# Two adjacency products of a graph layer as Strassen's seven half-size products, with features on partitions

## The chip, the cores and the metric

One core of a Trainium2 chip. The metric is device time of one execution in microseconds (us). "The profile" is a page that sums up one profiled execution. "The trace" is the record behind it, asked by views: groups of instructions, timeline, busy time by windows, waits. Times such as 1536.40 are us from the start of the profiled span.

## The reference

Two pre-norm residual layers over the rows of `x` [3327, 512] with an adjacency `adj` [3327, 3327], all in float32. Layer 0 is attention with `adj` added to the scores. The change is in layer 1:

```python
h = relu(layernorm(x1))
A2 = adj + eye(N)
s = diag(A2) ** -0.5
temp = A2 @ h @ W.T                       # first adjacency product, then the weights
out = x1 + relu((s[:, None] * A2 * s[None, :]) @ temp)    # second adjacency product
```

Each adjacency product is 3327 x 3327 by 3327 x 512. I call them convolution 1 and convolution 2.

## The kernel before

Layer 1 reads 128 x 512 tiles of the transposed adjacency from DRAM and never holds more than twelve of them. Its right sides, `h1` and `ts`, stay on chip. Convolution 1 leaves features on partitions; convolution 2 leaves rows on partitions, so its result goes straight to the output.

```python
def chunk(j, b, diagonal):                # A2^T[row tile j, column block b]
    a = conv.tile([P, BW], F32, name="a", bufs=12)
    load(a[:m, :wd], adjT[j * P : j * P + m, b * BW : b * BW + wd], m)
    ...                                   # + identity on the diagonal blocks
# (A2 h1)^T
for b in range(NB):
    acc = [psum.tile([P, BW], F32, name="mm", bufs=4) for _ in range(DC)]
    for j in range(NT):
        a = chunk(j, b, True)
        for d in range(DC):
            nc.tensor.matmul(acc[d][:, :wd], h1(j)[:, d, :], a[:m, :wd],       # L300
                             start=j == 0, stop=j == NT - 1)
        if j == 1 and waiting:
            temp(*waiting)                # ts of the block before, hidden in this one
    ...
# S A2 ts, and the residual
for b in range(NB):
    ...
    for j in range(NT):
        a = chunk(j, b, False)
        for t, i in enumerate(its):
            nc.tensor.matmul(acc[t][:n], a[:m, t * P : t * P + n], ts[j][:m],  # L324
                             start=j == 0, stop=j == NT - 1)
    ...
    for t, i in enumerate(its):           # scale and relu, residual, store
        ...
        store(out[i * P : i * P + n], r[:n], n)
```

Everything the second stage needs is on chip when the first ends, and the weights product `temp` of each block hides among the matmuls of the next. That is why TensorE hardly ever stops.

Of the kernel before, what the change touches and what calls it, by code (L numbers as in the profile page):

```python
# [9 lines left out]
F32 = mybir.dt.float32  # L10
# [5 lines left out]
BW = 512  # columns of a block: four row tiles, one PSUM bank of float32  # L16
# [4 lines left out]
def graph_layers_kernel(  # L21
# [4 lines left out]
    adjT: bass.AP,  # L26
# [6 lines left out]
    w1T: bass.AP,  # L33
    out: bass.AP,
):
    """Two pre-norm residual layers over the rows of x [N, D].

    Layer 0: x1 = x + softmax(q k^T / sqrt(D) + adj + adj) v, with h = relu(layernorm(x)).
    Layer 1: out = x1 + relu(S A2 S (A2 h1 W^T)), with A2 = adj + I, S = diag(A2)^-1/2.

    adjT and w*T are the transposes of adj and the weights; bq and bk come as [128, D / 128].
    All matrix products are in float32.
    """
# [3 lines left out]
    NT = (N + P - 1) // P  # row tiles  # L47
    NB = (N + BW - 1) // BW  # blocks of four row tiles
    TB = BW // P
    scale = 1.0 / math.sqrt(D)  # L50
# [10 lines left out]
    def pieces(n):  # L61
        # a DMA spreads over 16 engines only if 16 divides its partitions
        m = n - n % 16
        return [(0, m), (m, n)] if m and m < n else [(0, n)]
# [10 lines left out]
    held = ctx.enter_context(tc.tile_pool(name="held", bufs=1))  # L75
    work = ctx.enter_context(tc.tile_pool(name="work", bufs=2))
# [12 lines left out]
    # Per block, in turn: h^T of layer 0, q^T (scaled), h of layer 1. All three take  # L89
    # [128, 4, 128] for each row tile, and a row tile's earlier content is dead when the  # L90
    # next one is written.
# [3 lines left out]
    def h1(i):  # L95
        b, t = divmod(i, TB)
        return qh[b][: rows(i), :, t * P : (t + 1) * P]

    x1d = [dram.tile([rows(i), D], F32, name=f"x1d{i}") for i in range(NT)]

    def layernorm(dst, src, n):
        """dst = (src - mean) / sqrt(var + eps) along the row"""
# [10 lines left out]
    with tc.tile_pool(name="kv", bufs=1) as kv:  # L113
# [65 lines left out]
        S = {}  # L179

        def scores(i):
            """exp(a - max a) for the rows of tile i, in chunks of BW keys, and their negated max and sums"""
# [48 lines left out]
        def attend(i):  # L231
# [13 lines left out]
            y = work.tile([P, D], F32, name="y", bufs=1)  # L245
            layernorm(y[:n], xt[:n], n)
            nc.scalar.activation(h1(i), y[:n].rearrange("p (c e) -> p c e", c=DC), AF.Relu)
# [7 lines left out]
        att.close()  # L255

# [1 line left out]
    with tc.tile_pool(name="conv", bufs=1) as conv:  # L258
        w1 = conv.tile([P, DC, D], F32, name="w1")
        nc.sync.dma_start(w1, w1T.rearrange("(c p) o -> p c o", p=P))  # L260
        ts = [conv.tile([P, D], F32, name=f"ts{i}") for i in range(NT)]
        dg = [conv.tile([P, 1], F32, name=f"dg{i}") for i in range(NT)]
        sd = [conv.tile([P, 1], F32, name=f"sd{i}") for i in range(NT)]

        def chunk(j, b, diagonal):
            """A2^T[j-th row tile, b-th column block]"""
            m, wd = rows(j), width(b)
            a = conv.tile([P, BW], F32, name="a", bufs=12)
            load(a[:m, :wd], adjT[j * P : j * P + m, b * BW : b * BW + wd], m)
            if j // TB == b:  # L270
                t = j % TB
                blk = a[:m, t * P : t * P + m]
                nc.vector.tensor_add(blk, blk, ident[:m, :m])  # L273
                if diagonal:
                    junk = conv.tile([P, P], F32, name="junk", bufs=2)
# [3 lines left out]
            return a  # L279

        def temp(b, axt):
            """ts = S (A2 h1) W^T for the row tiles of block b"""
            for i in tiles_of(b):
                n, t = rows(i), i % TB
                ps = psum.tile([P, D], F32, name="av")
# [87 lines left out]
```

## Time and profile before

| | kernel before |
|---|---|
| time, median (lowest to highest, 4 runs) | 2798.26 us (2797.49 to 2799.17) |
| span of the profiled run | 2796.5 us |
| TensorE busy | 99% |
| convolution 1 starts / last matmul ends | 1536.4 / 2788.4 us |

The page, the seam between the layers and the end are shown in the prediction below. Windows over most of each convolution, kernel before; the columns are the stretch, its length, busy us (and count of instructions) of PE, PEld, DVE, ACT and POOL, then TensorE's clock, the DMA share and GB/s:

```profile
1600.00:2150.00 550.00, 550.00 (x1291) 245.35 (x1290) 35.40 (x93) 7.02 (x12) 10.96 (x20) 1.00 0.25 64
2210.00:2750.00 540.00, 540.00 (x1259) 239.33 (x1258) 23.85 (x46) 16.49 (x24) 13.03 (x24) 1.00 0.33 93
```

TensorE is busy in every microsecond at full clock. VectorE does 35 us of work in 550, and DMA is three quarters idle. The change wants to spend those idle resources to take work off TensorE.

### The profile page before, as it was taken

To read this page: it belongs to the slowest core of one execution; us is meant where nothing else is said; L and a number is where in the kernel's file an instruction comes from. 1 tells how busy PE (TensorE), PEld (TensorE's weight loads), DVE (VectorE), ACT (ScalarE), POOL (GpSimd) and SP (SyncE) were. 2 spreads that over 40 slices of the span, in tenths; PEclk is the share of its full clock that TensorE was granted. 3 is DMA by queue.
4 is the path that set the end of the run, shared out by engine and by line. 5 is a ranking of instruction groups with operands and counts; after the bars stand their busy time and mean duration, and the time that the engine had idled before them with its cause. 6 is when DMAs were issued, how large, how long until landed. Compare 5 with 4: busy or idle time off the path is not lost.

```text
span 2796.5 us, 18243 instructions
## 1 busy us (share of the span) xinstructions
PE 2770.7 (99%) x7260; PEld 1311.6 (47%) x7260; DVE 500.5 (18%) x979; ACT 255.7 (9%) x615; POOL 74.5 (3%) x138
## 2 busy tenths in 40 slices
PE   8999999999999999999998999999999999999998
PEld 4444544444444444454444444444445644444443
DVE  4121323232323232323222000000000000000000
ACT  1110111111111112121211000000000000000000
POOL 1000000000000000000000000000000000000000
PEclk9999999999999999999999999999999999999999
DMA  3000211111111211111111422222221332333322
GB/s 117 15 23 0 65 49 43 53 40 53 43 49 40 57 40 55 42 52 45 51 45 42 127 64 68 68 64 64 72 63 40 90 108 75 108 106 105 85 81 60
DMA packets 97045, 172.56 MB, mean 62 GB/s; under 512 B 11578, under 2 KB 21559, under 8 KB 96960
## 3 DMA queue, kind: packets, MB, share of 16 engines
q1 hardware_dynamic: 92736, 157.77, 20.5%
q0 software_dynamic: 4224, 13.63, 1.3%
q8 instruction: 57, 0.93, 0.1%
q14 instruction: 28, 0.23, 0.0%
HBM read 157.73 MB, written 13.63 MB: 61 GB/s over the span
## 4 chain that ended last, share of the span: by engine, by line
PE 99%; DMA 1%; DVE 0%; SPq 0%; ACT 0%; POOL 0%; issue 0%; POOLq 0%; ACTq 0%
PE mm L300 21%; PE av L242 21%; PE mm L198 21%; PE mm L324 21%; PE mm L158 6%; PE av L287 3%; PE av L151 3%; PE tp L223 3%; DMA xt<-in_x_dram 0%; PE tp L142 0%; DMA a<-in_adjT_dram 0%; DVE st L104 0%; DVE xt L111 0%; SPq L68 0%; ACT pT L225 0%
## 5 line engine op out<-in xcount | busy, mean ns | idle before, releaser
L242 PE MATMUL av<-v,pT 128*128 128x512 f32 (+2 forms) x1352 | 606.3, 593 | 0.6 <-ACT pT L225 0.6
L300 PE MATMUL mm<-a,qh 128*128 128x512 f32 (+3 forms) x1456 | 583.4, 563 | 7.6 <-DVE a L273 7.6
L198 PE MATMUL mm<-kT,qh 128*128 128x512 f32 (+3 forms) x1456 | 588.5, 562 | 0.0
L324 PE MATMUL mm<-ts,a 128*128 128x512 f32 (+2 forms) x1352 | 580.6, 592 | 0.0
L300 PEld LDWEIGHTS mm<-a,qh 128*128 128x128 f32 (+1 forms) x1456 | 277.7, 191 | 313.1 <-issue 307.6
L198 PEld LDWEIGHTS mm<-kT,qh 128*128 128x128 f32 (+1 forms) x1456 | 274.8, 190 | 302.6 <-issue 298.4
L324 PEld LDWEIGHTS mm<-ts,a 128*128 128x128 f32 (+2 forms) x1352 | 257.2, 190 | 322.7 <-issue 322.6
L242 PEld LDWEIGHTS av<-v,pT 128*128 128x128 f32 (+2 forms) x1352 | 246.8, 190 | 261.1 <-issue 253.8
L200 DVE SCALAR_TENSOR_TENSOR s<-s,mm 128x512 f32<-128x512 f32 (+2 forms) x182 | 118.2, 649 | 262.3 <-PE mm L198 262.3
L225 ACT COPY pT<-tp 128x512 f32<-128x512 f32 (+1 forms) x104 | 51.9, 499 | 819.2 <-PE tp L223 819.2
L208 ACT ACTIVATE s<-s,nmx 128x512 f32<-128x512 f32 (+2 forms) x182 | 123.2, 678 | 30.9 <-DVE nmx L204 30.2
L202 DVE TENSOR_REDUCE mx<-s 128x1 f32<-128x512 f32 (+2 forms) x182 | 117.9, 648 | 6.2
L223 PEld LDWEIGHTS tp<-ident,s 128*128 128x128 f32 (+2 forms) x676 | 84.8, 142 | 71.6 <-issue 68.8
L273 DVE TENSOR_TENSOR a<-a,ident 128x128 f32<-128x128 f32 (+1 forms) x52 | 15.2, 292 | 524.1 <-DMA a<-in_adjT_dram 432.9
L225 DVE COPY pT<-tp 128x512 f32<-128x512 f32 (+1 forms) x78 | 53.7, 688 | 269.6 <-PE tp L223 269.6
L223 PE MATMUL tp<-ident,s 128*128 128x128 f32 (+2 forms) x676 | 99.3, 273 | 0.0
L151 PE MATMUL av<-wv,qh 128*128 128x512 f32 (+1 forms) x208 | 93.1, 598 | 0.0
L158 PE MATMUL mm<-qh,wk 128*128 128x512 f32 (+1 forms) x224 | 90.4, 562 | 0.0
L158 PE MATMUL mm<-qh,wq 128*128 128x512 f32 (+1 forms) x224 | 90.4, 562 | 0.0
L287 PE MATMUL av<-w,axt 128*128 128x512 f32 (+1 forms) x208 | 90.4, 592 | 0.0
L332 ACT ACTIVATE r<-mm,sd 128x512 f32<-128x512 f32 (+1 forms) x26 | 17.9, 687 | 570.1 <-PE mm L324 570.1
L333 DVE TENSOR_TENSOR r<-r,x 128x512 f32<-128x512 f32 (+1 forms) x26 | 18.0, 693 | 283.8 <-ACT r L332 283.8
(40 smaller groups left out, 555.8 us busy)
## 6 DMA issues: line engine op xcount, KB each, us to landing
a<-in_adjT_dram SPq DMA_DIRECT2D x300, 256.0 KB, 2.7
s<-in_adj_dram SPq DMA_DIRECT2D x150, 256.0 KB, 2.7
xt<-in_x_dram SPq DMA_DIRECT2D x25, 256.0 KB, 3.3
xr<-in_x_dram SPq DMA_DIRECT2D x25, 256.0 KB, 2.7
x1d<-xr POOLq DMA_DIRECT2D x25, 256.0 KB, 2.3
x<-x1d SPq DMA_DIRECT2D x25, 256.0 KB, 4.1
out_dram<-r POOLq DMA_DIRECT2D x25, 256.0 KB, 5.1
a<-in_adjT_dram SPq DMA_DIRECT2D x50, 127.5 KB, 2.0
```

Source lines behind the costliest of these rows:

```text
L151: nc.tensor.matmul(ps[:n], qh[b][:, c, t * P : t * P + n], w["v"][:, c, :], start=c == 0, stop=c == DC - 1)
L158: nc.tensor.matmul(ps[:, :wd], w[nm][:, c, o * P : (o + 1) * P], qh[b][:, c, :wd], start=c == 0, stop=c == DC - 1)
L198: nc.tensor.matmul(ps[:n, :wd], qh[qb][:, d, t * P : t * P + n], kT[c][:, d, :], start=d == 0, stop=d == DC - 1)
L200: nc.vector.scalar_tensor_tensor(ch[c][:n, :wd], ch[c][:n, :wd], 2.0, ps[:n, :wd], op0=ALU.mult, op1=ALU.add)
L202: nc.vector.reduce_max(mx[:n, c : c + 1], ch[c][:n, :wd], axis=AX.X)
L208: nc.scalar.activation(ch[c][:n, :wd], ch[c][:n, :wd], AF.Exp, bias=nmx[:n], accum_out=sums[:n, c : c + 1])
L223: nc.tensor.transpose(pt[:m, k, :n], S[i][0][c][:n, k * P : k * P + m], ident[:n, :n])
L225: cp(sb[:, :full, :n], pt[:, :full, :n])
L242: nc.tensor.matmul(ps[:n], now[:m, k, :n], v[j][:m], start=j == 0, stop=j == NT - 1)
L287: nc.tensor.matmul(ps[:n], axt[:, d, t * P : t * P + n], w1[:, d, :], start=d == 0, stop=d == DC - 1)
L300: nc.tensor.matmul(acc[d][:, :wd], h1(j)[:, d, :], a[:m, :wd], start=j == 0, stop=j == NT - 1)
L324: nc.tensor.matmul(acc[t][:n], a[:m, t * P : t * P + n], ts[j][:m], start=j == 0, stop=j == NT - 1)
```

## The change

Pad N to 3328 and cut the matrices into quarters. Strassen's scheme then needs seven products of half size for eight, at the price of sums of the operands. VectorE makes those sums. The rows of the result are done in four strips of 416 columns per half. `adjq` is the padded transpose, cut on the host so that a strip of a quarter is contiguous. The diagonal, too, now comes cut from the host (`dg`); the kernel before took it from its tiles with VectorE. The time of the host is not measured. Features are on partitions in both convolutions, so convolution 2's result must be turned back. A right side is now needed as whole quarters before the first product can start, so `h1`, `ts` and both results go through DRAM.

```diff
-        def chunk(j, b, diagonal): ...
+        Y = {r: conv.tile([P, HT, HD], F32, name=f"y{r}") for r in range(1, 8)}
+        def right_sides(src):
+            for r, J, d in ((5, 1, 1), (2, 0, 0), (6, 0, 1), (3, 0, 1), (7, 1, 0), (4, 1, 0)):
+                nc.sync.dma_start(Y[r], quarter(src, J, d))
+            nc.vector.tensor_add(Y[6], Y[6], Y[2])
+            nc.vector.tensor_add(Y[1], Y[2], Y[5])
+            nc.vector.tensor_sub(Y[3], Y[3], Y[5])
+            nc.vector.tensor_add(Y[7], Y[7], Y[5])
+            nc.vector.tensor_sub(Y[4], Y[4], Y[2])
+        def strip(I, J, ch):          # 416 columns of a quarter, in four groups of row tiles
+            ... a = conv.tile([P, GMAX, CW], F32, name="a", bufs=10) ...
+        def combine(op, to, by):      # VectorE, group by group
+            ...
+        def product(xs, r):           # 2 x 13 matmuls, 416 wide
+            ... nc.tensor.matmul(acc[:, :CW], Y[r][:, g, d * P : (d + 1) * P], a[:, g - g0, :], ...)
+        def convolve(outT, after_first):
+            for ch in range(CH):
+                a11 = strip(0, 0, ch)
+                x = strip(0, 1, ch); combine(ALU.add, x, a11);      m = product(x, 5) ...
+                if ch > 0: after_first(ch)
+                x = strip(1, 0, ch); combine(ALU.subtract, x, a11); m = product(x, 6) ...
+                x = strip(1, 1, ch); combine(ALU.add, x, a11);      m = product(x, 1) ...
+                m = product(a11, 3) ...
+                ...                    # 7, 2 and 4 likewise, around a22
+        right_sides(h1d)
+        convolve(y1T, lambda ch: None)
+        for i in [*range(HT, NT), *range(HT)]:      # temp: now a stage of its own
+            o = columns_of(y1T, i) ...               # load, 4 matmuls with w1, scale
+            nc.gpsimd.dma_start(tsd[i * P : (i + 1) * P], t)
+        right_sides(tsd)
+        def finish(ch):                              # turn back the row tiles of a strip
+            ... o = columns_of(y2T, i)               # 3 buffers "ot"; "x1" and "r" have 2
+            ... nc.tensor.transpose(pt[:, d, :], o[:, d, :], ident) ...
+        convolve(y2T, lambda ch: finish(ch - 1))
+        finish(CH - 1)
```

(Joined and cut. `h1` of layer 0 now goes to `h1d`, a store from the GpSimd queue.)

More of the change, by code (lines that the diff above doesn't have):

```diff
@@ L25, in graph_layers_kernel @@
     adj: bass.AP,
-    adjT: bass.AP,
+    adjq: bass.AP,
     wqT: bass.AP,
@@ L33, in graph_layers_kernel @@
     w1T: bass.AP,
+    dg: bass.AP,
     out: bass.AP,
@@ L49, in graph_layers_kernel @@
     TB = BW // P
+    NP = NT * P
+    HT = NT // 2
+    HN = HT * P
+    HD = D // 2
+    CH = 4
+    CW = HN // CH
+    GROUPS = [(0, 4), (4, 7), (7, 10), (10, 13)]
+    GMAX = 4
     scale = 1.0 / math.sqrt(D)
@@ L74, in graph_layers_kernel @@
     const = ctx.enter_context(tc.tile_pool(name="const", bufs=1))
-    held = ctx.enter_context(tc.tile_pool(name="held", bufs=1))
-    work = ctx.enter_context(tc.tile_pool(name="work", bufs=2))
+    layer0 = ExitStack()
+    held = layer0.enter_context(tc.tile_pool(name="held", bufs=1))
+    work = layer0.enter_context(tc.tile_pool(name="work", bufs=2))
     psum = ctx.enter_context(tc.tile_pool(name="psum", bufs=2, space=bass.MemoryType.PSUM))
@@ L93, in graph_layers_kernel @@
           for b in range(NB)]
-    def h1(i):
-        b, t = divmod(i, TB)
-        return qh[b][: rows(i), :, t * P : (t + 1) * P]
+    h1d = dram.tile([NP, D], F32, name="h1d")
+    tsd = dram.tile([NP, D], F32, name="tsd")
+    y1T = dram.tile([D, NP], F32, name="y1T")
+    y2T = dram.tile([D, NP], F32, name="y2T")
     x1d = [dram.tile([rows(i), D], F32, name=f"x1d{i}") for i in range(NT)]
@@ L245, in attend @@
             y = work.tile([P, D], F32, name="y", bufs=1)
+            z = work.tile([P, D], F32, name="z", bufs=2)
             layernorm(y[:n], xt[:n], n)
-            nc.scalar.activation(h1(i), y[:n].rearrange("p (c e) -> p c e", c=DC), AF.Relu)
+            if n < P:
+                nc.vector.memset(z[96:], 0.0)
+            nc.scalar.activation(z[:n], y[:n], AF.Relu)
+            nc.gpsimd.dma_start(h1d[i * P : (i + 1) * P], z)
             del S[i]
@@ L255, in graph_layers_kernel @@
         att.close()
+    layer0.close()
     with tc.tile_pool(name="conv", bufs=1) as conv:
@@ L260, in graph_layers_kernel @@
         nc.sync.dma_start(w1, w1T.rearrange("(c p) o -> p c o", p=P))
-        ts = [conv.tile([P, D], F32, name=f"ts{i}") for i in range(NT)]
-        dg = [conv.tile([P, 1], F32, name=f"dg{i}") for i in range(NT)]
-        sd = [conv.tile([P, 1], F32, name=f"sd{i}") for i in range(NT)]
-        def chunk(j, b, diagonal):
-            m, wd = rows(j), width(b)
-            a = conv.tile([P, BW], F32, name="a", bufs=12)
-            load(a[:m, :wd], adjT[j * P : j * P + m, b * BW : b * BW + wd], m)
-            if j // TB == b:
-                t = j % TB
-                blk = a[:m, t * P : t * P + m]
-                nc.vector.tensor_add(blk, blk, ident[:m, :m])
-                if diagonal:
-                    junk = conv.tile([P, P], F32, name="junk", bufs=2)
-                    nc.vector.scalar_tensor_tensor(junk[:m, :m], blk, 1.0, ident[:m, :m], op0=ALU.mult,
-                                                   op1=ALU.mult, accum_out=dg[j][:m])
-                    nc.gpsimd.tensor_tensor(sd[j][:m], dg[j][:m], mhalf[:m], op=ALU.pow)
-            return a
@@ L281, in temp @@
-        def temp(b, axt):
-            for i in tiles_of(b):
-                n, t = rows(i), i % TB
-                ps = psum.tile([P, D], F32, name="av")
-                for d in range(DC):
-                    nc.tensor.matmul(ps[:n], axt[:, d, t * P : t * P + n], w1[:, d, :],
-                                     start=d == 0, stop=d == DC - 1)
-                nc.vector.tensor_scalar(ts[i][:n], ps[:n], sd[i][:n], None, op0=ALU.mult)
-        waiting = None
-        for b in range(NB):
-            wd = width(b)
-            acc = [psum.tile([P, BW], F32, name="mm", bufs=4) for _ in range(DC)]
-            for j in range(NT):
-                m = rows(j)
-                a = chunk(j, b, True)
-                for d in range(DC):
-                    nc.tensor.matmul(acc[d][:, :wd], h1(j)[:, d, :], a[:m, :wd],
-                                     start=j == 0, stop=j == NT - 1)
-                if j == 1 and waiting:
-                    temp(*waiting)
-            axt = conv.tile([P, DC, BW], F32, name="axt", bufs=2)
-            for d in range(DC):
-                cp = nc.vector.tensor_copy if d % 2 else nc.scalar.copy
-                cp(axt[:, d, :wd], acc[d][:, :wd])
-            waiting = b, axt
@@ L311, in graph_layers_kernel @@
-        for b in range(NB):
-            its = tiles_of(b)
-            acc = [psum.tile([P, D], F32, name="mm", bufs=4) for _ in its]
-            res = []
-            for i in its:
-                xr = conv.tile([P, D], F32, name="x1", bufs=8)
-                load(xr, x1d[i], rows(i))
-                res.append(xr)
-            for j in range(NT):
-                m = rows(j)
-                a = chunk(j, b, False)
-                for t, i in enumerate(its):
-                    n = rows(i)
-                    nc.tensor.matmul(acc[t][:n], a[:m, t * P : t * P + n], ts[j][:m],
-                                     start=j == 0, stop=j == NT - 1)
-                if j == 1 and waiting:
-                    temp(*waiting)
-                    waiting = None
-            for t, i in enumerate(its):
-                n = rows(i)
-                r = conv.tile([P, D], F32, name="r", bufs=4)
-                nc.scalar.activation(r[:n], acc[t][:n], AF.Relu, scale=sd[i][:n])
-                nc.vector.tensor_add(r[:n], r[:n], res[t][:n])
-                store(out[i * P : i * P + n], r[:n], n)
+        sd = conv.tile([P, NT], F32, name="sd")
@@ new lines, in graph_layers_kernel, with quarter @@
+        nc.sync.dma_start(sd, dg)
+        nc.vector.tensor_scalar(sd, sd, 1.0, None, op0=ALU.add)
+        mh = conv.tile([P, NT], F32, name="mh")
+        nc.vector.memset(mh, -0.5)
+        nc.gpsimd.tensor_tensor(sd, sd, mh, op=ALU.pow)
+        Y = {r: conv.tile([P, HT, HD], F32, name=f"y{r}") for r in range(1, 8)}
+        def quarter(src, J, d):
+            return src[J * HN : (J + 1) * HN, d * HD : (d + 1) * HD].rearrange("(t p) e -> p t e", p=P)
+        def right_sides(src):
[6 more added lines that the diff above has]
+            nc.vector.tensor_sub(Y[4], Y[4], Y[2])
@@ new lines, in strip @@
+        def strip(I, J, ch):
+            made = []
+            for g0, g1 in GROUPS:
+                a = conv.tile([P, GMAX, CW], F32, name="a", bufs=10)
+                nc.sync.dma_start(a[:, : g1 - g0], adjq[J, I, ch, g0:g1].rearrange("g p w -> p g w"))
+                if I == J:
+                    for g in range(g0, g1):
+                        lo, hi = max(g * P, ch * CW), min((g + 1) * P, (ch + 1) * CW)
+                        if lo < hi:
+                            blk = a[:, g - g0, lo - ch * CW : hi - ch * CW]
+                            nc.vector.tensor_add(blk, blk, ident[:, lo - g * P : hi - g * P])
+                made.append(a)
+            return made
@@ new lines, in combine @@
+        def combine(op, to, by):
+            for (g0, g1), a, b in zip(GROUPS, to, by):
+                n = g1 - g0
+                nc.vector.tensor_tensor(a[:, :n], a[:, :n], b[:, :n], op=op)
+        def product(xs, r):
+            ps = []
+            for d in range(2):
+                acc = psum.tile([P, BW], F32, name="mm", bufs=4)
+                for (g0, g1), a in zip(GROUPS, xs):
+                    for g in range(g0, g1):
+                        nc.tensor.matmul(acc[:, :CW], Y[r][:, g, d * P : (d + 1) * P], a[:, g - g0, :],
+                                         start=g == 0, stop=g == HT - 1)
+                ps.append(acc)
+            return ps
@@ new lines, in convolve, with first, more, done @@
+        def convolve(outT, after_first):
+            for ch in range(CH):
+                C = {k: conv.tile([P, 2, CW], F32, name="c", bufs=6) for k in (11, 12, 22)}
+                def first(k, ps, scale=1.0):
+                    for d in range(2):
+                        nc.scalar.activation(C[k][:, d, :], ps[d][:, :CW], AF.Copy, scale=scale)
+                def more(k, ps, op=ALU.add):
+                    for d in range(2):
+                        nc.vector.tensor_tensor(C[k][:, d, :], C[k][:, d, :], ps[d][:, :CW], op=op)
+                def done(k):
+                    I, dh = divmod(k - 11, 10)
+                    rows_ = outT[dh * HD : (dh + 1) * HD, I * HN + ch * CW : I * HN + (ch + 1) * CW]
+                    nc.sync.dma_start(rows_.rearrange("(d p) w -> p d w", p=P), C[k])
+                a11 = strip(0, 0, ch)
+                x = strip(0, 1, ch)
+                combine(ALU.add, x, a11)
+                m = product(x, 5)
+                first(11, m, -1.0)
+                first(12, m)
+                if ch > 0:
+                    after_first(ch)
+                x = strip(1, 0, ch)
+                combine(ALU.subtract, x, a11)
+                m = product(x, 6)
+                first(22, m)
+                x = strip(1, 1, ch)
+                combine(ALU.add, x, a11)
+                m = product(x, 1)
+                more(11, m)
+                more(22, m)
+                m = product(a11, 3)
+                more(12, m)
+                done(12)
+                more(22, m)
+                a22 = strip(1, 1, ch)
+                x = strip(0, 1, ch)
+                combine(ALU.subtract, x, a22)
+                m = product(x, 7)
+                more(11, m)
+                x = strip(1, 0, ch)
+                combine(ALU.add, x, a22)
+                m = product(x, 2)
+                C[21] = conv.tile([P, 2, CW], F32, name="c", bufs=6)
+                first(21, m)
+                more(22, m, ALU.subtract)
+                done(22)
+                m = product(a22, 4)
+                more(11, m)
+                done(11)
+                more(21, m)
+                done(21)
@@ new lines, in columns_of @@
+        def columns_of(src, i):
+            o = conv.tile([P, DC, P], F32, name="ot", bufs=3)
+            nc.sync.dma_start(o, src[:, i * P : (i + 1) * P].rearrange("(c p) e -> p c e", p=P))
+            return o
+        right_sides(h1d)
+        convolve(y1T, lambda ch: None)
+        for i in [*range(HT, NT), *range(HT)]:
+            o = columns_of(y1T, i)
+            ps = psum.tile([P, D], F32, name="av")
+            for d in range(DC):
+                nc.tensor.matmul(ps, o[:, d, :], w1[:, d, :], start=d == 0, stop=d == DC - 1)
+            t = conv.tile([P, D], F32, name="t", bufs=3)
+            nc.vector.tensor_scalar(t, ps, sd[:, i : i + 1], None, op0=ALU.mult)
+            nc.gpsimd.dma_start(tsd[i * P : (i + 1) * P], t)
@@ new lines, in graph_layers_kernel @@
+        right_sides(tsd)
+        def finish(ch):
+            for l in range(HT):
+                if (l * P + P - 1) // CW != ch:
+                    continue
+                for i in (l, HT + l):
+                    n = rows(i)
+                    xr = conv.tile([P, D], F32, name="x1", bufs=2)
+                    load(xr, x1d[i], n)
+                    o = columns_of(y2T, i)
+                    pt = psum.tile([P, DC, P], F32, name="tp")
+                    for d in range(DC):
+                        nc.tensor.transpose(pt[:, d, :], o[:, d, :], ident)
+                    r = conv.tile([P, D], F32, name="r", bufs=2)
+                    nc.scalar.activation(r, pt, AF.Relu, scale=sd[:, i : i + 1])
+                    nc.vector.tensor_add(r[:n], r[:n], xr[:n])
+                    store(out[i * P : i * P + n], r[:n], n)
@@ L349, in columns, with quartered, padded_diagonal @@
         return np.ascontiguousarray(np.asarray(a).reshape(-1, P).T)
+    def quartered(a):
+        a = np.asarray(a)
+        n = -(-len(a) // (2 * P)) * 2 * P
+        full = np.zeros((n, n), a.dtype)
+        full[: len(a), : len(a)] = a.T
+        full = full.reshape(2, n // (2 * P), P, 2, 4, n // 8)
+        return np.ascontiguousarray(full.transpose(0, 3, 4, 1, 2, 5))
+    def padded_diagonal(a):
+        d = np.diagonal(np.asarray(a))
+        full = np.zeros(-(-len(d) // P) * P, d.dtype)
+        full[: len(d)] = d
+        return np.ascontiguousarray(full.reshape(-1, P).T)
     ins = {
@@ L353 @@
         "adj": plain(adj),
-        "adjT": turned(adj),
+        "adjq": quartered(adj),
         "wqT": turned(L0_gnn_Wq),
@@ L361 @@
         "w1T": turned(L1_gnn_W),
+        "dg": padded_diagonal(adj),
     }
```

## The prediction

The forecast's sum came to 143.8 - 111 = 33 us, that is 2765, and 2770 with the 4 to 5 us for small waits. A term of 1.5 us, a delay between a load's last data and its use, is cut once from (a) and once from (b): no trace shows it. The sums are as they were made, so 1582 and +45.6 at (a), and 26.1, 27.6, 24 us idle and +29.5 at (b), still contain it: 3 of the 111 us.

The rest of the figures can be had from measured ones. 349.2 ns is an estimate: the point at width 416 on the straight line through the two spacings of the trace, 215.0 ns at 255 and 429.2 at 512. 381 GB/s for the 1664 B rows of a strip lies in the same way between the two packets that the trace timed. 3.7 us for a group to land is an estimate too: the page's 2.7 us for 256 KB, and the 0.38 MB more at 381 GB/s. The 693 ns of L333 are for 128x512, the 292 of L273 for 128x128. How 1891 ns, 1457 ns and 3.62 us for VectorE's longer additions were come by is cut; a straight line through those two gives 1896, 1462 and 3634, and the trace of the kernel after shows 1892 ns at 128x1664, 1457 at 128x1248 and 3.62 us at 128x3328.

> **What bounds the kernel now.** I read the page first (busy shares, chain of work, groups by shape), then the timeline at the two places where TensorE stops, then the windows view in 2 us stretches.
>
> ```profile
> PE 2770.7 (99%) x7260; PEld 1311.6 (47%) x7260; DVE 500.5 (18%) x979; ACT 255.7 (9%) x615; POOL 74.5 (3%) x138
> ...
> PE mm L300 21%; PE av L242 21%; PE mm L198 21%; PE mm L324 21%; PE mm L158 6%; PE av L287 3%; PE av L151 3%; PE tp L223 3%; DMA xt<-in_x_dram 0%; PE tp L142 0%; DMA a<-in_adjT_dram 0%; DVE st L104 0%; DVE xt L111 0%; SPq L68 0%; ACT pT L225 0%
> ...
> L300 PE MATMUL mm<-a,qh 128*128 128x512 f32 (+3 forms) x1456 | 583.4, 563 | 7.6 <-DVE a L273 7.6
> L324 PE MATMUL mm<-ts,a 128*128 128x512 f32 (+2 forms) x1352 | 580.6, 592 | 0.0
> L287 PE MATMUL av<-w,axt 128*128 128x512 f32 (+1 forms) x208 | 90.4, 592 | 0.0
> ```
>
> TensorE is the whole chain. L300 and L324 are the two adjacency products, 21% each, some 584 us each. TensorE idles before them once, for 7.6 us. Everything else is slack: VectorE is busy 18%. So work taken off TensorE is worth its full time, and every new wait of TensorE costs its full length. The two places where it stops now, the layers' seam and the end:
>
> ```profile
> 1528.88 0.39 SPq L260 DMA_DIRECT2D w<-in_w1T_dram  x1
> 1528.89 0.75 DVE L243 SCALAR_TENSOR_TENSOR xr<-av,rs,xr 127x512 f32<-127x512 f32 x1 [8.06 <-PE av L242]
> ...
> 1532.24 0.63 ACT L247 ACTIVATE qh<-y 127x512 f32<-127x512 f32 x1 [8.08 <-DVE y L111]
> 1536.01 0.29 DVE L273 TENSOR_TENSOR a<-a,ident 128x128 f32<-128x128 f32 x1 [3.80 <-DMA a<-in_adjT_dram]
> ...
> 1536.40 23.98 PE L300 MATMUL mm<-a,qh 128*128 128x512 f32 x51 [7.55 <-DVE a L273]
> ```
>
> At the seam the norm of the last row tile (done at 1532.9) is not waited for: TensorE starts with earlier row tiles as soon as the first adjacency tile is in.
>
> ```profile
> 2769.74 18.62 PE L324 MATMUL mm<-ts,a 128*128 128x512 f32 x43
> ...
> 2790.16 1.06 POOL L72 DMA_DIRECT2D out_dram<-r  x2 [0.32 <-DVE r L333]
> ```
>
> The span ends at 2796.5, 8.1 us after the last matmul. The third stretch is what a DMA burst and a cold clock look like:
>
> ```profile
> 1536.00:1538.00 2.00, 1.60 (x2) 0.83 (x3) 1.43 (x7) 0.00 (x0) 1.17 (x2) 0.50 1.06 408
> 1538.00:1540.00 2.00, 2.00 (x4) 0.72 (x3) 0.94 (x6) 0.00 (x0) 1.21 (x2) 0.50 1.05 406
> ```
>
> The last three numbers are the clock (0.50), the DMA share and GB/s. So about 400 GB/s is the ceiling for rows of 2 KB. The trace's DMA records give 84 ns for a packet of 2048 B and 46 ns for one of 1020 B: over 16 engines, 390 and 355 GB/s.
>
> [...] Here a float32 matmul is two instructions, and the timeline has 64 of width 512 in 27.47 us, 429.2 ns each, and 192 of width 255 in 41.28 us, 215.0 ns each[...], and shows the weight load (190 ns) hidden even at 255. [...] (clock 0.50 for 6.8 us after the 7.55 us gap, so 3.4 us of work lost). [...] the trace has 693 (L333) and 292 (L273).[...]
>
> **What is removed.** Strassen has seven half-size products for eight. Each product is 2 x 13 matmuls of width 416 per strip, 52 instructions of an estimated [...]349.2 ns: 18.16 us. Two convolutions x four strips x seven are 56 products, 1016.8 us. Before, L300 has 1248 instructions of 512 and 208 of 255 (1248 x 429.2 + 208 x 215.0 ns = 580.3 us), L324 has 1352 x 429.2 = 580.3; the chain's 21% each say the same. **Gain 1160.6 - 1016.8 = 143.8 us.** It is the eighth that Strassen promises; the padding (3328 for 3327 rows) costs nothing.
>
> **What is added beside TensorE.** Per strip (127 us of TensorE), VectorE has five combinations of 1891 + 3 x 1457 ns (31.3 us), 16 reads of PSUM of 416, estimated at 0.59 us between the trace's 421 ns for 255 and 688 for 512 (9.4 us), and 12 diagonal adds of 0.29: 44 us, 35%. Seven strips of 2.77 MB in 127 us are 153 GB/s of some 381. Buffers: ten, four of them held by the first quarter, six to work with; the third and fourth group of the next operand get a buffer 6.3 and 4.2 us before a product ends, need some 3.7 us to land and 1.5 to combine, and are wanted 4.9 us after its start. That leaves some 5 us of slack, so **I take no wait inside a convolution.**
>
> **What is added on the path.** (a) *The seam.* The first right side needs the last row tile of h1, which now goes through DRAM, and the load queue works in order: w1, the six quarters, then the strips. The order of instructions shows w1 waiting for all of layer 0's stores. From before's times: relu done 1532.9, store landed some 2.8 us later (x1d: 2.3 us), w1 issued 1536, data flows from 1537.4 (1.4 us later, as at 1528.9). Then 1.05 MB at 390 (2.7 us), 6 x 1.70 MB in 1 KB rows at 355 (28.8), the first quarter's strip 2.77 MB at 381 (7.3), one group 0.85 MB (2.2),[...] combination 1.9: TensorE starts at 1582, not 1536.4. **+45.6 us**; the five additions of 3.62 us hide under the loads. (b) *Between the convolutions.* temp keeps its time (104 matmuls, 89.3 us, before 90.4) but is now a stage by itself. Its loads look two tiles ahead (6.9 us against 3 to 4), and the quarters fetched in its midst may cost some 2 us. After its last matmul: eviction 0.8, store 3, 1.4 to first data, three quarters 5.1 MB 14.4 us[...], then the additions in order, Y3's last at 26.1, and the combination of the third group, 27.6. TensorE has 3.5 us of the next product left to do meanwhile: **24 us idle plus 3.4 of cold clock, with the 2 of temp: +29.5.** (c) *Turning back.* 26 tiles x 4 transposes at 0.16 us (0.64 per four in the timeline); 18 of the tiles fall inside convolution 2, 11.5 us, and I add 1.5 us per batch of six for two-deep buffers: **+16.** (d) *The end.* After the last product come a 1.3 us eviction, a store, a load (some 3 us each), then eight tiles through two output buffers, so in four pairs, each held by ACT 0.7, DVE 0.7, the issue 0.6 and a store of 2.3 us or more, some 4.5 us: 7.3 + 1 of transposes + 4 x 4.5 = 26, and up to 30 with slower stores, against 8.1; I take 28. **+20.** The sum: 45.6 + 29.5 + 16 + 20 = 111 us of new path; the cold start at (a) is there before too. Net 143.8 - 111 = 33 us, that is 2798 - 33 = 2765. Built forward from the seam it is the same: 1582 + 3.4 + 508.5 + 91.5 + 27.5 + 507 + 16 + 28 = a span of 2764, and time stands 1.7 us over span. With 4 to 5 us for small waits I do not see, I say **2770**: most of the gain is eaten by the seams.
>
> **Rivals.** *R1, the gain arrives nearly whole (2640 to 2700):* the loads at the seams would have to be hidden. For: DMA is mostly idle. Against: the load queue is in order and stands behind the last store. *R2, the convolutions starve (2850 and more):* VectorE works strictly in order and mixes combinations that wait for loads with evictions; 2 us per product is +112. For: each product wants a new 2.77 MB operand through six free buffers. Against: the 5 us of slack above, VectorE at 35%. *R3, same sum, other split:* 1 KB rows load at 250 rather than 355 GB/s: +12 at (a) and +6 at (b), 2788; or stores take 5 us (out_dram's median on the page is 5.1): +12 at the end.
>
> **Range and chances.** R3's terms both against me give about 2800; loads at 390 and a tail of 20 give 2752. R1 I hold at 5%, R2 at 4%: faster by over 2% (below 2742) 0.06, slower (above 2854) 0.04, within 2% 0.90.
>
> **What would show it.** Right: 416-wide matmuls 349 ns apart, a product every 18.2 us with no gap inside; TensorE's first idle some 53 us at the seam, released by a VectorE combination with DMA near 100%; a second of about 24 us after temp; a tail of some 28 us of alternating ACT, DVE and stores; VectorE about 35% in layer 1. Wrong: idle TensorE before each product (R2), or a seam under 20 us (R1).

## The result, and the profile after

| | before | after |
|---|---|---|
| time, median of 4 runs | 2798.26 us | 2771.29 us (2768.78 to 2772.09) |
| ratio to before, 95% interval | | 0.9902 (0.9888 to 0.9916) |
| span of the profiled run | 2796.5 us | 2767.0 us |
| TensorE busy | 2770.7 us | 2650.9 us |
| VectorE busy | 500.5 us | 841.2 us |
| DMA packets | 97,045 | 201,830 |

Ratios here are the mean time of one kernel's runs over that of the other's in the same rounds, so not quite the ratio of the medians quoted. The kernel is 27 us faster, though TensorE's busy time fell by 120 us. Groups of the kernel after; L326 is the Strassen product, L318 the combination of strips, L400 `temp`, L418 the turning back:

```profile
L326 PE MATMUL mm<-a,y 128*128 128x416 f32 x2912 | 1026.4, 515 | 60.0 <-DVE a L318 54.1 <-DVE y L294 5.9
...
L318 DVE TENSOR_TENSOR a<-a 128x1248 f32<-128x1248 f32 x120 | 174.7, 1457 | 279.0 <-DMA a<-in_adjq_dram 168.4 <-PE mm L326 90.1 <-issue 18.9
...
L400 PE MATMUL av<-w,ot 128*128 128x512 f32 x208 | 90.3, 593 | 4.7 <-DMA ot<-y1T 4.2 <-DVE t L402 0.5
...
L418 PE MATMUL tp<-ident,ot 128*128 128x128 f32 x104 | 20.4, 341 | 23.7 <-DMA ot<-y2T 18.0 <-ACT r L420 5.6
```

Before, L300 and L324 were busy 583.4 + 580.6 = 1164.0 us; L326 is busy 1026.4. Its 2912 matmul instructions (56 products of 52) wait only twice in all: 54.1 us at the seam, released by a combination, and 5.9 us before product 6 of convolution 2, released by an addition of right sides. The windows by stage, kernel after:

```profile
1540.00:1560.00 20.00, 0.00 (x0) 0.00 (x0) 7.14 (x3) 0.00 (x0) 4.51 (x1) 0.50 1.08 350
1583.35:2092.00 508.65, 508.65 (x1452) 276.69 (x1453) 168.72 (x191) 15.68 (x32) 0.00 (x0) 1.00 0.53 168
2092.00:2185.00 93.00, 88.29 (x207) 38.80 (x206) 28.55 (x31) 0.00 (x0) 12.99 (x24) 1.00 0.66 216
...
2220.00:2700.00 480.00, 470.56 (x1384) 257.76 (x1384) 162.99 (x188) 24.28 (x44) 9.71 (x18) 0.99 0.58 183
2700.00:2767.00 67.00, 36.67 (x113) 20.77 (x111) 8.88 (x14) 6.53 (x10) 4.85 (x9) 0.73 0.33 105
```

The second line is the insides of convolution 1: not a microsecond of idle TensorE, VectorE at 33%. The first line is what that is paid with: TensorE idle, DMA saturated at 350 GB/s. The seam in the timeline, to be held against the seam of before (`1536.40 23.98 PE L300 ...`):

```profile
1533.53 0.62 POOL L262 DMA_DIRECT2D h1d<-z  x1 [1.54 <-ACT z L261]
...
1537.25 23.16 SPq L293 DMA_DIRECT2D y<-h1d  x6
...
1551.84 3.62 DVE L295 TENSOR_TENSOR y<-y,y 128x3328 f32<-128x3328 f32 x1 [9.58 <-DMA y<-h1d]
1556.67 3.62 DVE L294 TENSOR_TENSOR y<-y,y 128x3328 f32<-128x3328 f32 x1 [1.20 <-DMA y<-h1d]
1560.45 19.78 SPq L305 DMA_DIRECT2D a<-in_adjq_dram  x10
...
1581.15 3.26 DVE L318 TENSOR_TENSOR a<-a 128x1664 f32<-128x1664 f32 x2 [5.48 <-DMA a<-in_adjq_dram]
1583.35 26.87 PE L326 MATMUL mm<-a,y 128*128 128x416 f32 x71 [54.12 <-DVE a L318]
```

The last row tile's `h1` goes out at 1533.5. The queue then brings the weights, all six quarters (the additions start 4.9 us apart, so 1.70 MB per 4.9 us = 348 GB/s) and only then the strips. The second seam, after `temp`, in TensorE's and VectorE's lines:

```profile
2094.89 1.46 DVE L318 TENSOR_TENSOR a<-a 128x1248 f32<-128x1248 f32 x1 [0.19 <-DMA a<-in_adjq_dram]
...
2189.78 16.92 PE L326 MATMUL mm<-a,y 128*128 128x416 f32 x48
...
2201.84 3.63 DVE L295 TENSOR_TENSOR y<-y,y 128x3328 f32<-128x3328 f32 x1 [11.11 <-DMA y<-tsd]
...
2208.92 3.62 DVE L294 TENSOR_TENSOR y<-y,y 128x3328 f32<-128x3328 f32 x1
2212.59 27.64 PE L326 MATMUL mm<-a,y 128*128 128x416 f32 x70 [5.89 <-DVE y L294]
```

Product 5 follows `temp` with no wait at all: the last of its four combinations is the first line, at 2094.9, early in `temp` (four of its 52 instructions even ran inside `temp`). It covers most of the loads and additions. Last, turning back inside convolution 2 (first two lines) and the end (the rest), kernel after:

```profile
2346.39 1.89 SPq L390 DMA_DIRECT2D ot<-y2T  x3
2353.01 0.63 PE L418 MATMUL tp<-ident,ot 128*128 128x128 f32 x4 [2.98 <-DMA ot<-y2T]
...
2734.47 1.09 PE L418 MATMUL tp<-ident,ot 128*128 128x128 f32 x4 [6.35 <-DMA ot<-y2T]
2741.26 0.69 ACT L420 ACTIVATE r<-tp,sd 128x512 f32<-128x512 f32 x1 [3.43 <-DMA out_dram<-r]
2755.96 1.06 POOL L84 DMA_DIRECT2D out_dram<-r  x2 [2.09 <-DVE r L421]
```

The last product ends at 2728.1, the last store is issued at 2755.96, the span ends at 2767.0. The 11.0 us from the last issue to the end were 6.3 before (2790.16 to 2796.5).

### The profile page after: what moved, and what is told of

Read it like the earlier page. It is cut to its first block, busy times and chain, and to the rows that moved or that the text cites. A ratio compares the mean times of both kernels' runs of the same rounds, so it can differ in the third digit from the quotient of the medians. Undisturbed runs are those within 1.5% of the kernel's fastest.

```text
span 2767.0 us, 19101 instructions
## 1 busy us (share of the span) xinstructions
PE 2650.9 (96%) x7468; PEld 1345.0 (49%) x7468; DVE 841.2 (30%) x1258; ACT 278.4 (10%) x665; POOL 92.7 (3%) x165
## 2 busy tenths in 40 slices
DMA packets 201830, 300.48 MB, mean 109 GB/s; under 512 B 11640, under 2 KB 162935, under 8 KB 201740
## 3 DMA queue, kind: packets, MB, share of 16 engines
q0 software_dynamic: 8384, 27.27, 2.5%
## 4 chain that ended last, share of the span: by engine, by line
PE 72%; issue 23%; DMA 1%; SPq 1%; POOL 1%; DVE 0%; POOLq 0%; ACT 0%; ACTq 0%; DVEq 0%
PE mm L209 21%; PE av L253 20%; PE mm L326 18%; PE mm L169 6%; PE av L162 3%; PE tp L234 3%; SPq L293 1%; DMA a<-in_adjq_dram 1%; PE av L400 1%; DMA xt<-in_x_dram 0%; POOL out_dram L84 0%; POOL tsd L403 0%; PE tp L153 0%; SPq L305 0%; DVE st L115 0%
## 5 line engine op out<-in xcount | busy, mean ns | idle before, releaser
L326 PE MATMUL mm<-a,y 128*128 128x416 f32 x2912 | 1026.4, 515 | 60.0 <-DVE a L318 54.1
L326 PEld LDWEIGHTS mm<-a,y 128*128 128x128 f32 x2912 | 555.2, 191 | 524.0 <-issue 509.2
L318 DVE TENSOR_TENSOR a<-a 128x1248 f32<-128x1248 f32 (+1 forms) x160 | 248.6, 1566 | 349.0 <-DMA a<-in_adjq_dram 236.5
L338 ACT ACTIVATE c<-mm 128x416 f32<-128x416 f32 x64 | 31.3, 516 | 1099.1 <-PE mm L326 1099.1
L342 DVE TENSOR_TENSOR c<-c,mm 128x416 f32<-128x416 f32 x128 | 70.6, 583 | 195.5 <-PE mm L326 118.5
L400 PE MATMUL av<-w,ot 128*128 128x512 f32 x208 | 90.3, 593 | 4.7 <-DMA ot<-y1T 4.2
L254 DVE SCALAR_TENSOR_TENSOR xr<-av,rs,xr 128x512 f32<-128x512 f32 (+1 forms) x26 | 19.5, 751 | 209.0 <-PE av L253 209.0
L177 DVE TENSOR_SCALAR qh<-mm,bq_sb 128x512 f32<-128x512 f32 (+1 forms) x28 | 19.8, 712 | 155.8 <-PE mm L169 153.9
## 6 DMA issues: line engine op xcount, KB each, us to landing
y<-tsd SPq DMA_DIRECT2D x6, 1664.0 KB, 12.5
```

Of the source, the lines that this page charges most:

```text
L318: nc.vector.tensor_tensor(a[:, :n], a[:, :n], b[:, :n], op=op)
L326: nc.tensor.matmul(acc[:, :CW], Y[r][:, g, d * P : (d + 1) * P], a[:, g - g0, :], start=g == 0, stop=g == HT - 1)
L400: nc.tensor.matmul(ps, o[:, d, :], w1[:, d, :], start=d == 0, stop=d == DC - 1)
```

## The experiments

All are compared with the kernel before in the same rounds. All gave correct results.

**e1_front: load what is needed first.** The theory: the seam is a matter of order in one queue, not of bandwidth alone. The first product needs one quarter and two strips, and six quarters and the weights stand before them.

```diff
-            for r, J, d in (...six quarters...): load; five additions
+            fetch(src, 5)                    # then strips a11, x
+            ...combine...; fetch(src, 2, 6)  # then strip of product 6
+            ...combine...; fetch(src, 3, 7, 4); load w1
```

> Change: at the start of each convolution the loads are issued in the order of need: the quarter of the first product, then the two strips of the first product, then the other quarters; w1 last. The bytes ahead of the first product fall from 13.9 to 5.3 MB (quarter 1.7, strip 2.8, one group 0.85). Theory (the seam is the bytes that stand in the load queue ahead of the first product, at some 350 GB/s): TensorE starts about 25 us earlier, 1558 instead of 1583; time 2744 (2738 to 2750). Between the convolutions the addition that the second product waits for comes first, up to 4 us of this. Rival (the seam is the round trip store, load, addition and their latencies): less than 8 us, 2763 or more.

Measured: 2752.28 us, ratio 0.9836 (0.9821 to 0.9851), so 19 us under the changed kernel, 2 us above the range expected; the four runs lie between 2748.2 and 2757.2, and the profiled one is the slowest. The timeline of e1_front:

```profile
1556.46 39.37 PE L320 MATMUL mm<-a,y 128*128 128x416 f32 x104 [26.91 <-DVE a L312]
...
1573.93 9.11 SPq L292 DMA_DIRECT2D y<-h1d  x3
1583.09 4.80 SPq L403 DMA_DIRECT2D w<-in_w1T_dram  x1
1588.00 10.14 SPq L299 DMA_DIRECT2D a<-in_adjq_dram  x6
...
1601.79 23.53 PE L320 MATMUL mm<-a,y 128*128 128x416 f32 x60 [5.96 <-DVE a L312]
```

TensorE starts 26.9 us earlier, as expected. Some 9 us were given back: two products later the strip of product 1 stands behind three quarters and the weights in the same queue, TensorE waits 5.96 us, and runs at half clock for the 4.7 us after that (convolution 1 lasts 519.8 us for 510.3). In this profiled run convolution 2 lost another 5 us, an estimated 3 of them to longer cold periods: the matmuls of both convolutions are busy 1032.9 us for 1026.4, and convolution 1 has some 3.5 of these 6.5 (its 9.5 us less the wait). The order of the queue is the seam's cause, and an order has to be right for each product, not only for the first.

**e2_plain8: same layout, eight plain products.** This parts the two things the change does. All of the new layout stays (strips, quarters through DRAM, turning back); the sums and the seventh-for-eighth go. Two quarters and one strip fewer stand before the first product.

```diff
-                x = strip(0, 1, ch); combine(ALU.add, x, a11); m = product(x, 5) ... (seven)
+                for I in (0, 1):
+                    e = strip(I, 1, ch); f = strip(I, 0, ch)
+                    product(e, 5); product(f, 6)     # right half of the features
+                    product(e, 7); product(f, 2)     # left half
```

> Change: everything of the changed kernel stays (turned, quarters, through DRAM, four strips, transposes at the end), but the seven products with combinations are eight plain products, summed as before in the output buffers. TensorE gets 8 more products of 18.16 us, +145; two quarters of 1.7 MB fewer at each seam, -10, no additions at the second seam, -6. Theory (TensorE is the bound inside the convolutions, so an eighth is worth its whole time): 2900 (2890 to 2910). Rival (combinations and their waits take back much of the eighth inside the convolutions): the difference to the changed kernel is under 100 us, below 2865.

Measured: 2885.43 us, ratio 1.0309 (1.0294 to 1.0325), 5 us under the range expected. Convolution 1 in the timeline of e2_plain8:

```profile
1563.52 584.00 PE L320 MATMUL mm<-a,y 128*128 128x416 f32 x1664 [34.70 <-DMA a<-in_adjq_dram]
```

The layout by itself costs 2885.4 - 2798.3 = 87 us, and the eighth product is worth 2885.4 - 2771.3 = 114 us in it, net of the loads and additions that Strassen adds at the seams. By stage: convolution 1 took 583.8 us for 510.3, 73.5 us for four more products of 18.16 us (72.6); convolution 2 took 64.9 us more, for it lost the 5.9 us wait and the cold clock that follows. The seam was 19.4 us shorter, where I had expected 10. Strassen's eighth is paid out in full inside the convolutions; the layout around it takes three quarters of it back.

**e3_double: each combination done twice.** The rival theory, R2 of the prediction, is that VectorE's in-order stream is close to starving TensorE. (That it works in order the trace of the kernel after shows: at 1784.60 VectorE began to wait for a load, a product's last matmul ended at 1785.2, the load came at 1786.02 and was combined, and only at 1787.40 did VectorE read the product.) Doubling its combinations (the second pass is a maximum of a value with itself, so the result stays right) would then cost nearly its own length.

```diff
                 nc.vector.tensor_tensor(a[:, :n], a[:, :n], b[:, :n], op=op)
+                nc.vector.tensor_tensor(a[:, :n], a[:, :n], a[:, :n], op=ALU.max)
```

> Change: each combination on VectorE is followed by one of the same size on the same tile (the maximum of the tile with itself; the result stays right), 250 us more VectorE work, VectorE in layer 1 from about 34% to 58%. Theory (combinations lie beside TensorE with some 5 us of slack per operand): +0 to +6 us, 2771 to 2777, of which 2 at the start of the first product. Rival (the convolutions hang on VectorE and its order): each of the 40 operands delays TensorE by 1.5 us or more, 2830 or more.

Measured: 2786.29 us, ratio 0.9959 (0.9942 to 0.9976), 15 us over the changed kernel, between the two theories but far nearer the first. The window over convolution 1, e3_double:

```profile
1584.00:2101.00 517.00, 511.55 (x1454) 276.84 (x1455) 290.15 (x273) 15.68 (x32) 0.00 (x0) 0.99 0.53 165
```

VectorE went from 169 us to 290 us, and TensorE idles 4.8 us inside convolution 1, in five waits of 0.5 to 2 us, each <-DVE a (the window's other 0.6 us lie before the first matmul). About 250 us of added VectorE work (the group L318 of 250 us once more) cost 15, more than the 0 to 6 of the theory. So VectorE doesn't bound the convolutions, but the extra 6.2 us per operand are enough to use the slack up in places. The slack itself can be read from the instruction records of the kernel after, combinations and matmuls paired in order: the tightest group of an operand is ready 4.8 us before the first matmul that reads it (median of the 40 operands; 3.1 us at least, but for the first operand after the seam).

**e4_tail: more buffers at the end.** The last eight row tiles take their input, residual and output tiles from the strips' ten buffers, which are free by then. The theory: the pairs of the prediction's (d), each waiting for a store to land, set the tail.

```diff
-                    xr = conv.tile([P, D], F32, name="x1", bufs=2)
+                    if ch == CH - 1:
+                        big = conv.tile([P, GMAX, CW], F32, name="a", bufs=10)...
+                        xr, r, o = three slices of big
```

> Change: the last eight row tiles take their input, residual and output out of the strips' ten buffers, which are free by then, so none waits for another's store. Measured: 38.9 us from the last product to the end. Theory (two output and two residual buffers set the tail's pace): eight tiles then follow each other at about 1.1 us, the tail falls to some 26 us, time 2758 (2754 to 2763). Rival (the tail is the store, load and store latencies and the program's end): under 4 us gained, 2767 or more.

Measured: 2764.19 us, ratio 0.9877 (0.9863 to 0.9892), a gain of 7 us where I had expected 13. The last store is issued 23.4 us after the last product ends, not 27.9; the tail is 34.4 us for 38.9. So buffers are the smaller part. What stays are about 6.5 us for a store and a load of the last strip, loads that follow one another at some 2 us, and 11 us after the last issue that no buffer changes.

**e5_split: turn back three and three.** Six row tiles at once run out of three `ot` and two `x1` buffers, and TensorE, where the next product stands behind these transposes, waits for the fourth's load. Split, the second three load under the next product.

```diff
-                if ch > 0: after_first(ch)          # six tiles after product 5
+                if ch > 0: after_first(ch, 0)       # three after product 5
                 ... m = product(x, 6)
+                if ch > 0: after_first(ch, 1)       # three after product 6
```

> Change: the six row tiles that are turned back inside each strip of the second convolution are split: three after the first product, three after the second, so that the second three have a whole product for their loads. Theory (TensorE idles 3.1 us per strip, three times, because these loads are issued only when the first three buffers are free): 9.5 us of idle time and some cold clock go, time 2760 (2757 to 2763). Rival (another wait takes their place, the two output buffers): 2768 or more.

Measured: 2756.14 us, ratio 0.9848 (0.9833 to 0.9862), so 15 us gained where 11 were expected. Convolution 2 takes 524.9 us for 538.3. Group of the transposes, e5_split (L418 in the kernel after, where it had 23.7 us of idle):

```profile
L421 PE MATMUL tp<-ident,ot 128*128 128x128 f32 x104 | 18.5, 322 | 14.7 <-DMA ot<-y2T 9.2 <-ACT r L423 5.4
```

The 9 us of idle that went are the three waits of 3 us. What is left lies in the tail. The clock records show most of the rest: in the kernel after two of the three batches were followed by 3.4 us at half clock, here none. (The two profiled runs differ by 12.5 us; the medians' 15 includes that the profiled run of the kernel after is its fastest.)

**e8_act: the new stores from ScalarE's queue.** After the last issue the kernel after needs 11.0 us where the kernel before needs 6.3. The trace's instruction records have a closing drain of GpSimd of 9.37 us in the one and 5.12 us in the other. GpSimd issues 106 DMAs against 54; the 52 more are the stores of `h1` and `ts`. The theory: the drain grows with the number of DMAs that GpSimd issued.

```diff
-            nc.gpsimd.dma_start(h1d[i * P : (i + 1) * P], z)
+            nc.scalar.dma_start(h1d[i * P : (i + 1) * P], z)
-            nc.gpsimd.dma_start(tsd[i * P : (i + 1) * P], t)
+            nc.scalar.dma_start(tsd[i * P : (i + 1) * P], t)
```

> Change: the stores of h1 and of ts are issued by ScalarE instead of GpSimd; GpSimd issues 54 instead of 106 DMAs, as in the kernel before. Measured: GpSimd's last drain takes 9.37 us (5.12 in the kernel before) and ends the span, long after the last store has landed. Theory (the drain grows with the DMAs that GpSimd has issued): it falls to some 5.1 us, time 2767 (2764 to 2769). Rival (the drain depends on what is in flight at the end): it stays at 9.4, time 2771.

Measured: 2763.38 us, ratio 0.9878 (0.9863 to 0.9893), 8 us under the changed kernel; the drain is 5.122 us again, to the nanosecond that of before. The waits of the sync engine at the very end, kernel before, kernel after, e8_act:

```profile
SPq L369 <- PEq L369: 3.0, 2, 2.5
```

```profile
SPq L475 <- PEq L475: 7.9, 2, 7.0
```

```profile
SPq L475 <- PEq L475: 3.0, 2, 2.5
```

(us in total, times, longest.) The view names TensorE's queue as the releaser, which had long been done; what lasts in that time in the records is GpSimd's drain. Only the drain is explained. The two profiled runs differ by 6.6 us: 4.7 in the tail, 1.2 in convolution 2, 0.8 before convolution 1. `temp` isn't shorter: its own waits fall from 4.7 to 0.6 us, but two instructions of product 5 that run inside it now wait 3.5 us for right sides. Number and bytes of the DMAs (13.63 MB for 27.27) changed together here, so which of them counts is not shown.

**e6_all, e7_best, e9_few: together.** e6_all joins e1, e4 and e5.

> Change: order of loads (measured alone -19 us), tail out of free buffers (-7) and the split of the turning back (expected -11) together. Theory (these lie one after the other on TensorE's path, so they add): 2734 (2729 to 2740), 2.3% under the kernel before. Rival (each uncovers the next wait): 2745 or more.

Measured: 2731.9 us, ratio 0.9763 (0.9747 to 0.9779). The parts add.

e7_best also takes e8's stores and mends e1's order: quarters 7 and 4 are fetched after the strip of product 1, the weights later still, and the first half of `ts` comes in two loads, so that part of it doesn't wait for the last row tile.

> Change: as the one with all three, and: the right sides of the later products are loaded behind the strips of the third product (the run with the new order waited 6.0 us there and ran cold afterwards), the first half's ts is fetched in two parts, the larger before the last row tiles are stored, and ScalarE issues the stores of h1 and ts. Theory: a further 8 us at the first seam, 6 to 9 at the second (TensorE waited 5.9 us there for an addition, then ran cold), 4 at the end: 2715 (2708 to 2724), about 3% under the kernel before. Rival: the waits reappear elsewhere, 2730 or more.

Measured: 2711.21 us, ratio 0.9688 (0.9674 to 0.9703). Convolution 1 takes 510.1 us and convolution 2 516.4, with no wait of TensorE inside either; 2.6 us <-DMA y<-tsd fall on two instructions of product 5 that run inside `temp`. The transposes in convolution 2 now cost 516.4 less its 1454 instructions at 349.2 ns, 8.7 us, with no idle.

e9_few leaves only 18 DMAs to GpSimd (`x1` and the last strip's output go by ScalarE's queue).

> Change: as the best version so far (2711), but ScalarE also issues the stores of x1 and of the last eight row tiles, so that GpSimd issues 18 DMAs in all instead of 54. Theory (GpSimd's last drain is a fixed part and some 0.082 us for each DMA that it has issued, from 5.12 us at 54 and 9.37 us at 106): it falls to 2.2 us, and the time by 3 us, to 2708 (2705 to 2711). Rival (5.1 us is the least, or what counts is something else than the number): no change of the drain, 2711 or, where ScalarE's own order delays the tail, more.

Measured: 2706.43 us (2705.48 to 2708.25), ratio 0.9671 (0.9655 to 0.9687): the best version, 3.3% under the kernel before. The time was as expected, the drain was not: 3.54 us instead of 2.2, so it isn't a fixed part and 0.082 us for each DMA. It ran at 2594 us, after GpSimd's last store and far from the end. The tail is 26.7 us for 29.6 in e7_best, and `temp` 95.0 for 98.8. Windows of e9_few: the seam, convolution 1, `temp`, convolution 2, the tail:

```profile
1530.00:1556.00 26.00, 1.19 (x2) 0.84 (x3) 5.46 (x12) 0.63 (x1) 5.04 (x2) 0.54 0.85 293
1556.00:2064.00 508.00, 508.00 (x1451) 276.14 (x1450) 185.39 (x195) 15.68 (x32) 0.00 (x0) 1.00 0.59 186
2064.00:2163.00 99.00, 95.49 (x223) 41.58 (x222) 30.05 (x33) 0.00 (x0) 0.00 (x0) 1.00 0.74 242
2163.00:2680.00 517.00, 514.00 (x1520) 281.79 (x1518) 183.76 (x204) 26.83 (x50) 9.94 (x18) 1.00 0.57 180
2680.00:2703.70 23.70, 8.70 (x32) 5.73 (x32) 5.54 (x8) 5.50 (x8) 0.00 (x0) 0.50 0.83 269
```

Left over are a seam of 26 us and a tail of 27 us. The seam is one quarter and two strips in a row, at 293 GB/s over the window. The strips depend on nothing in layer 0, but they could not be loaded earlier without space that layer 0's buffers hold; I did not try that.

## Why the prediction was right, point by point

The total was off by 1.3 us. That is better than its parts deserve. Stage by stage, us:

| stage | predicted | measured | off by |
|---|---|---|---|
| TensorE starts layer 1 | 1582 | 1583.4 | +1.4 |
| convolution 1 | 511.9 | 510.3 | -1.6 |
| temp | 91.5 | 96.1 | +4.6 |
| convolution 2, with the second seam and turning back | 550.5 | 538.3 | -12.2 |
| tail to the end of the span | 28 | 38.9 | +10.9 |
| span | 2764 | 2767.0 | +3 |

The 5 us "for small waits" covered the rest. Two terms of ten microseconds and more were wrong with opposite signs: that they cancelled was luck.

- **The gain, 143.8 us: right.** The product is 18.16 us as worked out (349.2 ns from start to start of the warm instructions), and e2 shows the eighth paid at 73.5 us per four.
- **"No wait inside a convolution": right in convolution 1, and nearly so in 2.** The load and combination of each operand hide. The reason given, some 5 us of slack per operand, holds: 4.8 us is the median in the trace, and e3 shows waits when each combination takes twice as long.
- **(a) The seam: right in sum and in mechanism.** The idle is 54.1 us, released by a combination; 1 KB rows came at 348 GB/s for the 355 assumed. The sum holds the 1.5 us that are cut. e1 and e2 show that it is order in the queue: 27 and 19 us of it go when less stands ahead.
- **(b) Between the convolutions: wrong, 27.5 us of idle and cold clock predicted, 8.9 measured** (5.9 of wait and half of the 6.0 us that were cold after it). The step that failed is "the combination of the third group, 27.6". I had put product 5's third group behind the additions in VectorE's order. The trace has all its groups combined by 2096.4, 93 us before `temp` ended, since those strips depend on nothing in `temp` (even two groups of product 6 were, by 2102.5): product 5 ran through, and 16.9 us of it covered what I had as idle, where I had counted "3.5 us of the next product". The first addition came when the prediction's terms put it, the cut 1.5 us among them: 2201.8, 12 us into the seam.
- **temp: under by 4.6 us.** The look-ahead of two tiles doesn't hide all loads beside the strips' traffic: 4.7 us of wait for some 2 allowed, 4.2 of it <-DMA ot. Another 1.4 us are the four instructions of product 5.
- **(c) Turning back: 16 predicted, 22.3 measured** (538.3 less the 1452 instructions left to it, 507.1, less 8.9). Right in mechanism, wrong in both terms: transposes cost 8.7 (as in e7), not 11.5 us, and the two-deep buffers cost 9.4 us of idle for 4.5, with some 3 us of cold clock after; about 1 us stays unassigned. e5 removes the idle and the cold clock.
- **(d) The tail: mis-sized, 38.9 for 28.** The last store is issued 27.9 us after the last product, where (d)'s own terms put it at about 24 (7.3 + 1 + three pairs of 4.5 + 2 of the fourth): +4. From there to the end (d) had the other 4 us, and it took 11.0. Some 2 of those 7 I could have read from the kernel before, which took 6.3; 4.25 are GpSimd's longer drain, of which I had no notion, a side effect of moving `h1` and `ts` to DRAM through that queue. e8 shows it.
- **The cold clock at the seam.** The 3.4 us "of work lost" in the kernel before were 1.9: of the 6.8 us at half clock only 3.7 fell after TensorE restarted. In the clock records after, low periods last 3.413, 6.827 or a larger multiple of 3.413 us (54.6 at the first seam; the last one runs to the end), and of the 6.8 us at the second seam 6.0 fell after the restart. What a wait of 3 us costs is not fixed: of three of 2.94 to 3.00 us one cost nothing, and the other two were followed by 3.4 us at half clock. The records allow more. In each of the two traces, before and after, all low periods start on one grid of 3.413 us. Cut along it, from 30 us on, all seven full-clock pieces in which TensorE idled 2.04 us or more were followed by half clock, and none with 1.64 or less. The harmless wait was split by the grid into 1.64 and 1.34 us; the pieces of the other two held 2.04 and 2.46. So in these traces the loss was a matter of where the wait fell on the grid. Why the clock keeps one is not shown.
- **Rivals.** R1 failed in the kernel as changed, but e7 and e9 show what spoke for it: half of the seams' cost was order and buffers. R2 is ruled out by the window of convolution 1 and by e3. R3's slow rows didn't come, and its slow stores neither (the output's landed in 3.4 us, the median on the page).

So the small result has a settled cause. Between the profiled runs, 29.5 us apart, the bill closes: 143.8 us saved; given back 47.0 at the first seam (the later start), 5.4 in `temp`, 8.9 at the second seam, 22.3 in turning back and 30.8 at the end, 114.4 in all. e2 draws the line elsewhere: the eighth net of its own loads, 114, against the layout, 87.

## What to carry to other kernels

A scheme that saves TensorE work also decides when operands must be whole; count the seams it makes (loads and a cold clock: 47.0 us at the first here, 8.9 at the second) before counting the products it saves. In one load queue that works in order (here the quarters were issued from 1537.3, the strips behind them from 1560.5), list the transfers ahead of each product, not only of the first, and see which strips need nothing from the stage before: those cover the seam. A sum that comes out right can hide errors of opposite sign, so check a prediction stage by stage.
